# Seven products of half-size blocks instead of eight, in the projections of three images of a four-layer network

## The chip, the core and the metric

The kernel runs on one core of one Trainium2 chip. The core has an engine for matrix products (TensorE, called PE in the profile, with a separate path PEld that loads weights), three engines for elementwise work (VectorE or DVE, ScalarE or ACT, GpSimd or POOL), and a queue engine (SyncE or SP) that here only starts transfers. All engines run at the same time, each through its own list of instructions, in the order of that list, and wait for one another by semaphores. TensorE writes its results to PSUM, a small memory of eight banks per partition; one bank holds 512 numbers in fp32 per partition. GpSimd doesn't read PSUM in this kernel.

The metric is the device time of one execution in microseconds. Before the change it was 2751.64 us, the median of three runs (2740.83, 2752.58 and 2751.64).

## What is computed

The input is four images of 512 channels and 32 x 32 = 1024 positions (tokens), in fp32. Four layers follow one another, each `x = x + layer(group_norm(x))`: a self-attention with mixed heads, a gate per channel, a second self-attention (the one that is changed here), and a lookup of the eight best of 2048 stored items. Cut to the second self-attention, the reference says:

```python
def _conv1x1(x, w, b):
    return jnp.einsum('bchw,oc->bohw', x, w) + b[None, :, None, None]
# x: 4 images, 512 channels, 32 x 32; NUM_HEADS = 8, D_K = 64
q = _conv1x1(x, Wq, bq)
k, v = jnp.split(_conv1x1(x, Wkv, bkv), 2, axis=1)
q, k, v = (t.reshape(b, NUM_HEADS, D_K, l) for t in (q, k, v))
attn = jax.nn.softmax(jnp.einsum('bhct,bhcs->bhts', q, k) * SCALE, axis=-1)
out = jnp.einsum('bhts,bhcs->bhct', attn, v).reshape(b, c, h, w)
out = _conv1x1(out, Wp, bp)
```

So each image needs four products of a 512 x 512 weight with a 512 x 1024 image: the projections Q, K, V before the attention and P after it.

## The kernel before

Layer 2 (the second self-attention, counted from zero) takes the images one after another. Image 0 gets its Q, K and V at the end of layer 0; for the other three they are made between two attentions. One product of a projection is 128 output rows by 512 columns, summed over four blocks of 128 channels in PSUM:

```python
def project(w, rhs, m, at, evacuate, name="proj"):
    ps = place(at, f"{name}_{m}")              # two banks of PSUM
    for n in range(T // NB):                   # T = 1024, NB = 512
        for k in range(KC):                    # KC = 4
            pin(nc.tensor.matmul(
                ps[:, n, :], w[:, k, m * P:(m + 1) * P], rhs(k, n),
                start=(k == 0), stop=(k == KC - 1)))
    evacuate(flat2(ps))
# Q: q = (ps + bq) * SCALE on VectorE     K: k = ps + bk on ScalarE
# V: v = ps + bv on VectorE, with bv2 = bv copied to all partitions
```

That is 4 x 2 x 4 = 32 matmuls for each projection. `pin` keeps an instruction in its place in the program; instructions without it may be moved by the scheduler of the kernel language.

The attention of an image goes in 16 units of four key blocks:

```python
def scores2(b, u, before=None):
    # four times: two matmuls -> sc (two banks), then exp2():
    #   e = places2[:, count[0] % 6]; nc.scalar.activation(e, sc, AF.Exp)
    # the third and fourth exp come within apply2 of the unit before
    # sums of the e tiles for the softmax denominators:
    #   nc.gpsimd.tensor_add(two, es[i], es[i + 1])
    #   nc.vector.tensor_add(I["es", m, n], I["es", m, n], two)
def apply2(b, u, exp2=None):   # eight matmuls v x e -> pv
def finish2(b):                # after two units: rs matmuls, copy, reciprocal, o = pv * ri
```

The way out of the layer, P, adds the residual, which has to come from DRAM in pieces of 128 x 512:

```python
def put_out2(b):
    def add_out(m, ps):
        st = small.tile([P, 2, 6], F32, tag="bnst", ...)
        for n in range(T // NB):
            xr = apool.tile([P, NB], F32, tag="xr", bufs=2, ...)
            nc.sync.dma_start(out=xr, in_=x1[b][:, m, n * NB:(n + 1) * NB])
            nc.scalar.activation(xr, xr, AF.Identity, bias=I["tb"]..., scale=s1...)
            nc.vector.tensor_add(xr, ps[:, n * NB:(n + 1) * NB], xr)
            nc.sync.dma_start(out=x2[b][:, m, n * NB:(n + 1) * NB], in_=xr)
            nc.vector.bn_stats(st[:, n, :], xr)
        nc.vector.bn_aggr(mv[:, m, :], ...)
    for m in range(KC):
        project(I["Wp"], tokens(I["o"]), m, None, lambda ps: add_out(m, ps), ...)
```

Only two pieces `xr` exist, so a third is loaded when the first has been stored. The order of the whole layer, with its buffers:

```python
ps_s = tc.tile_pool(name="ps_s2", bufs=3, space=PSUM)   # three tiles of two banks
ps_m = tc.tile_pool(name="ps_m2", bufs=2, space=PSUM)   # two tiles of one bank, for pv
# ... memT (the items of layer 3, 4 MB) is loaded here, before layer 2 begins
for b in range(B):
    for s, u in enumerate(UNITS2):                 # 16 units
        if s == 5 and not last: load2(b + 1)       # Wq, Wk, Wv of the next image
        if s >= 1: scores2(b, u, UNITS2[s - 1])
        # steps of the normalization of the next image (from s == 8) ...
    if not last:
        for m in range(KC): take_q2(b + 1, m)      # Q
        img[b]["Wp"] = load_w("Wp", ...)
    apply2(b, UNITS2[-1])
    if not last:
        for m in range(KC): take_k2(b + 1, m)      # K
    finish2(b)
    if not last:
        for i in range(TC // 2): take_v2(b + 1, i) # V
        scores2(b + 1, UNITS2[0])                  # first unit of the next image
    put_out2(b)                                    # P
```

The weights Wq, Wk, Wv and Wp share three places of 1 MB, taken in turn.

Of the kernel before, what the change touches and what calls it, by code (L numbers as in the profile page):

```python
# [16 lines left out]
P = 128  # L17
# [24 lines left out]
def fast_net(ctx: ExitStack, tc: tile.TileContext, a: dict, out: bass.AP, flag: bass.AP):  # L42
# [17 lines left out]
    def small_ps(name):  # L60
        return pt_bank
# [12 lines left out]
    bq2 = chan(a["bq"], "bq2")  # L74
    bk2 = chan(a["bk"], "bk2")
    bp2 = chan(a["bp"], "bp2")
    fcb = chan(a["fc_b"], "fcb")

    both = const.tile([P, C], F32, tag="fcw", name="fcw")
# [814 lines left out]

    count = [0]

    def prepare2(b, in_steps=False):
# [31 lines left out]
    def take_q2(b, m, at=None):  # L931
        I = img[b]
        if m == 0:
            I["q"] = big("q", f"q2_{b}")
        project(I["Wq"], tokens(I["xn"]), m, at, lambda ps: pin(nc.vector.tensor_scalar(
            I["q"][:, m, :], ps, bq2[:, m:m + 1], SCALE, ALU.add, ALU.mult)), f"q2_{b}")

    def take_k2(b, m, at=None):
        I = img[b]
# [5 lines left out]
    def take_v2(b, i, at=None):  # L945
        I = img[b]
        if i == 0:
            I["v"] = big("v", f"v2_{b}").rearrange("p k (i c) -> p (k i) c", c=C)
        project_tokens(
            I["Wv"], lambda k, t: I["xn"][:, k, t * P:(t + 1) * P], i, at,  # L950
            lambda ps: pin(nc.vector.tensor_add(
                I["v"][:, 2 * i:2 * i + 2, :], ps,
                bv2.rearrange("p c -> p () c").to_broadcast([P, 2, C]))), f"v2_{b}")

    def scores2(b, u, before=None):

# [7 lines left out]
        def exp2():  # L964
            e = places2[:, count[0] % 6]
            count[0] += 1
            nc.scalar.activation(e, scs[len(es)], AF.Exp)  # L967
            es.append(e)

        for i, t in enumerate(range(t0, t0 + 4)):  # L970
# [44 lines left out]
    def finish2(b):  # L1015
# [19 lines left out]
        for r in range(2):  # L1035
            i = 2 * ((b * KC + m) * (T // NB) + n) + r
            nc.gpsimd.dma_start(out=seen[i:i + 1, :], in_=ri[r * HD:r * HD + 1])

    def put_out2(b):
        I = img[b]  # L1040
        s1 = l2[b][1]
        mv = small.tile([P, KC, 2], F32, tag="mv", name=f"mv_d{b}")

        def add_out(m, ps):
            st = small.tile([P, 2, 6], F32, tag="bnst", name=f"st_d{b}_{m}")
            for n in range(T // NB):
                xr = apool.tile([P, NB], F32, tag="xr", bufs=2, name=f"xr_c{b}_{m}_{n}")
                nc.sync.dma_start(out=xr, in_=x1[b][:, m, n * NB:(n + 1) * NB])
                nc.scalar.activation(
                    xr, xr, AF.Identity, bias=I["tb"][:, m:m + 1], scale=s1[:, m:m + 1])  # L1050
                nc.vector.tensor_add(xr, ps[:, n * NB:(n + 1) * NB], xr)
                nc.sync.dma_start(out=x2[b][:, m, n * NB:(n + 1) * NB], in_=xr)
                nc.vector.bn_stats(st[:, n, :], xr)
            nc.vector.bn_aggr(mv[:, m, :], st.rearrange("p i s -> p (i s)"))

        for m in range(KC):
            project(I["Wp"], tokens(I["o"]), m, None, lambda ps: add_out(m, ps), f"p2_{b}")
        gc3 = const.tile([P, 2, KC], F32, tag=f"gc3_{b}", name=f"gc3_{b}")
        l3[b] = (mv, gc3)

# [189 lines left out]
    for b in range(B):  # L1250
# [22 lines left out]
            ks[m](at)  # L1273
        if last:
            run_out(instance_norm(b))
            bv2 = apool.tile([P, C], F32, tag="o2", name="bv2")
            nc.sync.dma_start(out=bv2, in_=a["bv"].partition_broadcast(P))
            for i, at in enumerate(("mx0", "mx1", "sc", "mx0")):
                take_v2(0, i, at)
            for m, at in enumerate(("mx1", "sc", "mx0", "mx1")):  # L1280
                put_out(b, m, at)
# [11 lines left out]
    places2 = eT_flat[:, 0:6 * 2 * NB].rearrange("p (i r q) -> p i r q", i=6, r=2)  # L1293
    sums2 = eT_flat[:, 6 * 2 * NB:8 * 2 * NB].rearrange("p (i r q) -> p i r q", i=2, r=2)
    pair_sum = e.rearrange("p i r qq k -> p i r (qq k)")
    memT = []
    for k in range(KC):
        if k < 2:
            m_ = apool.tile([P, NI], F32, tag="s2", bufs=2, name=f"memT{k}")
        else:  # L1300
            m_ = eT_flat[:, (4 + k) * NI:(5 + k) * NI]
        nc.sync.dma_start(out=m_, in_=a["memT"][k * P:(k + 1) * P, :])
        memT.append(m_)
    tiles = [(b, tt) for b in range(B) for tt in range(TC)]
    atts, picks, sums = {}, {}, {}
    scores2(0, UNITS2[0])
    for b in range(B):
# [4 lines left out]
        for s, u in enumerate(UNITS2):  # L1312
            if s == 5 and not last:
                load2(b + 1)
            if s == 5 and last:
                img[b]["Wp"] = load_w("Wp", f"Wp2_{b}")
            if s >= 1:
                scores2(b, u, UNITS2[s - 1])
            for _ in range(2):
                if s >= 3:  # L1320
                    next(behind, None)
                if s >= 8:
                    next(ahead, None)
        run_out(ahead)
        if not last:
            for m in range(KC):
                take_q2(b + 1, m)
            img[b]["Wp"] = load_w("Wp", f"Wp2_{b}")
        apply2(b, UNITS2[-1])
        if not last:  # L1330
            for m in range(KC):
                take_k2(b + 1, m)
        finish2(b)
        if last:
            atts[0] = attention(*tiles[0])
        else:
            for i in range(TC // 2):
                take_v2(b + 1, i)
            scores2(b + 1, UNITS2[0])
        put_out2(b)  # L1340

# [739 lines left out]
```

## Time and profile before

The profile is of one execution with a span of 2741.6 us. Line numbers (L...) are those of the kernel before.

| what | where in the profile | number |
|---|---|---|
| TensorE busy | first part of the page | 2593.0 us, 95% of the span |
| GpSimd busy | first part of the page | 1266.2 us, 46% |
| VectorE busy | first part of the page | 1522.8 us, 56% |
| one projection of 32 matmuls | chain of work, PE q, k, v L197/L209 | 27.66 us |
| from the start of Q to the first product of the values in the next image | chain of work, 1508.68 to 1641.24 | 132.6 us |
| the 16 units of an attention | chain of work, 1641.24 to 1745.93 | 104.7 us |
| sum of two e tiles on GpSimd, 128 x 1024 | groups of instructions, POOL L991 | 2412 ns |
| the same on VectorE | groups of instructions, DVE L992 | 1384 ns |

How to read it: the trace holds two records of a weight load and two of a matmul for each fp32 matmul of the program, so that a projection appears as 64 records. The chain of work is followed backwards from the last instruction of the program: at each step it goes to what released that instruction, or, if it waited for nothing, to the one before it on its engine. Where the chain stays on PE, only a shorter list of PE work makes the program shorter; where it leaves PE for a DMA or another engine, PE stood still.

### The profile page before, as it was taken

To read this page: it belongs to the slowest core of one execution; us is meant where nothing else is said; L and a number is where in the kernel's file an instruction comes from. 1 tells how busy PE (TensorE), PEld (TensorE's weight loads), DVE (VectorE), ACT (ScalarE), POOL (GpSimd) and SP (SyncE) were. 2 spreads that over 40 slices of the span, in tenths; PEclk is the share of its full clock that TensorE was granted. 3 is DMA by queue.
4 is the path that set the end of the run, shared out by engine and by line. 5 is a ranking of instruction groups with operands and counts; after the bars stand their busy time and mean duration, and the time that the engine had idled before them with its cause. 6 is when DMAs were issued, how large, how long until landed. Compare 5 with 4: busy or idle time off the path is not lost.

```text
span 2741.6 us, 46996 instructions
## 1 busy us (share of the span) xinstructions
PE 2593.0 (95%) x18286; PEld 1180.3 (43%) x18286; DVE 1522.8 (56%) x2386; ACT 1007.6 (37%) x1149; POOL 1266.2 (46%) x1955
## 2 busy tenths in 40 slices
PE   8988999989989898989999999999999999999995
PEld 3443544545445444545433433343343334444442
DVE  5487337871588526873235224513623537788886
ACT  0565336551565426552154025214502622121210
POOL 2266325552455514653067017305702735666664
PEclk9999999999999999999999999999999999999997
DMA  2577438880687627785310030021002016767665
GB/s 78 128 206 204 128 93 219 218 216 28 172 216 202 164 69 193 205 207 199 116 32 1 31 123 1 16 77 62 1 31 92 1 48 189 220 186 216 185 183 148
DMA packets 159321, 349.82 MB, mean 128 GB/s; under 512 B 32361, under 2 KB 65129, under 8 KB 155378
## 3 DMA queue, kind: packets, MB, share of 16 engines
q1 hardware_dynamic: 86304, 167.04, 21.2%
q0 software_dynamic: 51200, 142.93, 19.3%
q10 hardware_dynamic: 21586, 36.76, 4.6%
q8 instruction: 147, 2.41, 0.4%
q14 instruction: 84, 0.69, 0.1%
HBM read 178.57 MB, written 33.69 MB: 77 GB/s over the span
## 4 chain that ended last, share of the span: by engine, by line
PE 82%; DMA 7%; ACT 4%; DVE 2%; issue 1%; POOL 1%; SPq 1%; ACTq 0%; POOLq 0%; DVEq 0%
PE at L1094 16%; PE sc_c L973 7%; PE pv_c L1006 7%; PE sc L451 7%; PE mx L197 7%; PE pv L511 6%; PE pt L410 4%; DMA s<-ss 4%; PE p L197 4%; PE sc L197 4%; PE v L209 3%; PE k L197 3%; PE q L197 3%; PE pt L684 3%; ACT ss L457 2%; PE mx L471 2%
## 5 line engine op out<-in xcount | busy, mean ns | idle before, releaser
L484 DVE STREAM_TRANSPOSE eT<-e 128x1024 f32<-128x1024 f32 x256 | 317.6, 1242 | 273.9 <-ACT e L478 272.0
L464 POOL DMA_DIRECT2D s<-ss x512 | 259.8, 515 | 384.4 <-ACT ss L457 299.6
L1111 POOL DMA_INDIRECT got<-in_mem,ix x256 | 280.2, 1095 | 208.3 <-DVE tmx L1117 92.3
L457 ACT COPY ss<-sc 128x1024 f32<-128x1024 f32 x256 | 258.9, 1011 | 264.4 <-PE sc L451 212.7
L967 ACT ACTIVATE eT<-sc_c 128x1024 f32<-128x1024 f32 x256 | 247.9, 1021 | 275.3 <-PE sc_c L973 213.3
L500 DVE BATCH_NORM_STATS2 st<-e 128x6 f32<-128x256 f32 x1024 | 341.6, 406 | 0.0
L451 PE MATMUL sc<-k,q 64*32 64x512 f32 x4096 | 287.1, 617 | 22.5 <-ACT ss L457 17.6
L991 POOL TENSOR_TENSOR e<-eT 128x1024 f32<-128x1024 f32 x96 | 231.3, 2412 | 164.7 <-ACT eT L967 133.2
L478 ACT ACTIVATE e<-mx 128x1024 f32<-128x1024 f32 x256 | 262.5, 1029 | 65.5 <-PE mx L471 28.0
L992 DVE TENSOR_TENSOR eT<-eT,e 128x1024 f32<-128x1024 f32 x96 | 132.8, 1384 | 274.0 <-POOL e L991 274.0
L511 PE MATMUL pv<-eT,v 128*64 128x128 f32 x4096 | 256.5, 279 | 0.0
L973 PE MATMUL sc_c<-q,k 64*128 64x512 f32 x1024 | 243.2, 614 | 11.3 <-ACT eT L967 9.0
L511 PEld LDWEIGHTS pv<-eT,v 128*64 128x64 f32 x4096 | 226.1, 139 | 63.9 <-issue 62.3
L1006 PE MATMUL pv_c<-eT,v 128*64 128x512 f32 x1024 | 234.4, 600 | 0.0
L471 PE MATMUL mx<-s,wmix 32*32 32x512 f32 x4096 | 159.6, 625 | 45.0 <-DMA s<-ss 44.9
L1135 DVE SCALAR_TENSOR_TENSOR acc<-got,et,acc 128x512 f32<-128x512 f32 x224 | 168.4, 752 | 8.0
L1033 DVE RECIPROCAL ri_c<-ri_c 128x512 f32<-128x512 f32 x32 | 107.0, 3345 | 96.1 <-ACT ri_c L1032 96.1
L973 PEld LDWEIGHTS sc_c<-q,k 64*128 64x128 f32 x1024 | 94.9, 189 | 144.0 <-issue 74.7
L1099 ACT COPY att<-at 128x1024 f32<-128x1024 f32 x64 | 64.8, 1012 | 217.8 <-PE at L1094 217.6
L987 POOL TENSOR_TENSOR eT<-eT 128x1024 f32<-128x1024 f32 x32 | 76.0, 2374 | 147.0 <-ACT eT L967 146.8
L587 POOL TENSOR_TENSOR o<-pv,rb 64x256 f32<-64x256 f32 x128 | 111.1, 868 | 67.1 <-ACT pv L574 60.2
L1006 PEld LDWEIGHTS pv_c<-eT,v 128*64 128x64 f32 x1024 | 70.9, 138 | 155.2 <-issue 154.6
(317 smaller groups left out, 3325.5 us busy)
## 6 DMA issues: line engine op xcount, KB each, us to landing
s<-ss SPq DMA_DIRECT2D x512, 128.0 KB
s<-ss POOLq DMA_DIRECT2D x512, 128.0 KB, 4.4
rb<-r POOLq DMA_DIRECT2D x64, 128.0 KB, 5.9
o<-o SPq DMA_DIRECT2D x32, 256.0 KB
xr<-in_x ACTq DMA_DIRECT2D x32, 256.0 KB
x<-xr SPq DMA_DIRECT2D x32, 256.0 KB
xr_c<-x SPq DMA_DIRECT2D x32, 256.0 KB
x<-xr_c SPq DMA_DIRECT2D x32, 256.0 KB
```

The source lines that it names most:

```text
L197: pin(nc.tensor.matmul(ps[:, n, :], w[:, k, m * P:(m + 1) * P], rhs(k, n), start=(k == 0), stop=(k == KC - 1),))
L451: pin(nc.tensor.matmul(sc[m * NS:(m + 1) * NS, r, :], q[r * HD:(r + 1) * HD, m, s * NS:(s + 1) * NS], k_[r * HD:(r + 1) * HD, m, n * NB:(n ...
L457: pin(nc.scalar.copy(ss[:, :, n * NB:(n + 1) * NB], sc))
L464: pin(relays[r].dma_start(out=s2[r * KC + m::NH], in_=ss[m * NS:(m + 1) * NS, r, :]))
L478: pin(nc.scalar.activation(e[:, half].rearrange("p r qq k -> p (r qq k)"), flat2(pairs[f"mx{half}"]), AF.Exp))
L484: pin(nc.vector.transpose(eT[:, j % 2].rearrange("p b (qq i r) x -> p i r qq b x", qq=2, i=4)[:, i, 2 * half:2 * half + 2], e[:, half].rea ...
L500: pin(nc.vector.bn_stats(st[:, i, 2 * half + r, qq, :], e[:, half, r, qq, :]))
L511: pin(nc.tensor.matmul(pv[r * HD:(r + 1) * HD, gp, :], I["v"][:, t, g * HD:(g + 1) * HD], eT[:, j % 2, t, :, 4 * g:4 * g + 4], start=(t == ...
L973: pin(nc.tensor.matmul(sc[:, r, :], I["k"][r * HD:(r + 1) * HD, m, t * P:(t + 1) * P], I["q"][r * HD:(r + 1) * HD, m, n * NB:(n + 1) * NB] ...
L1006: pin(nc.tensor.matmul(pv[r * HD:(r + 1) * HD, :], I["v"][:, t, h * HD:(h + 1) * HD], e[:, r, :], start=(t == 0), stop=(t == TC - 1),))
L1094: pin(nc.tensor.matmul(sc[:, n * NB:(n + 1) * NB], xn3[b][:, k, tt * P:(tt + 1) * P], memT[k][:, i0:i0 + NB], start=(k == 0), stop=(k == K ...
L1111: pin(nc.gpsimd.indirect_dma_start(out=got[:, i, :], out_offset=None, in_=a["mem"], in_offset=bass.IndirectOffsetOnAxis(ap=ix[:, i:i + 1], ...
```

## The change

A product of 2 x 2 blocks can be had from seven products of blocks instead of eight, if sums of blocks are formed before and after (Strassen's form, here with the fifteen sums of Winograd's variant). The change uses this for the projections Q, K and V of the images 1 to 3 and P of the images 0 to 2. The weight is cut into four blocks of 256 x 256, the image into four of 256 x 512. The aim is fewer matmuls on TensorE: 28 instead of 32 for each projection. The sums of weight blocks go to GpSimd, those of image blocks and of results to VectorE.

Around it: SCALE moves from the evacuation of Q into the exp; the bias of V no longer is added to V but carried through Wp once (`carry_bias`, 16 small matmuls) into the bias of P; and the items of layer 3 are loaded late, since their place now holds sums of blocks. The core of the diff, cut where `...` stands:

```diff
+    def seven_w(w, nm):                     # blocks of 128 x (2 x 256) on GpSimd
+        s = apool.tile([P, NI], F32, tag="s2", bufs=2, name=f"s_{nm}")
+        s1, s2_, s4 = ( ... )
+        nc.gpsimd.tensor_add(s1, block(1, 0), block(1, 1))
+        nc.gpsimd.tensor_sub(s2_, s1, block(0, 0))
+        nc.gpsimd.tensor_sub(s4, block(0, 1), s2_)
+        nc.gpsimd.tensor_sub(block(1, 0), block(0, 0), block(1, 0))
+        return None, block(0, 0), block(0, 1), s4, block(1, 1), s1, s2_, block(1, 0)
+
+    def seven_x(x, places):                 # blocks of 128 x (2 x 512) on VectorE
+        t1, t2, t4 = places
+        nc.vector.tensor_sub(t1, block(0, 1), block(0, 0))
+        nc.vector.tensor_sub(block(0, 1), block(1, 1), block(0, 1))
+        nc.vector.tensor_sub(t2, block(1, 1), t1)
+        nc.vector.tensor_sub(t4, block(1, 0), t2)
+        return None, block(0, 0), block(1, 0), block(1, 1), t4, t1, t2, block(0, 1)
+
+    def seven(product, put, nm):
+        ag = ps_s.tile([P, 2, NB], F32, tag="sc", name=f"ag_{nm}")
+        de = ps_s.tile([P, 2, NB], F32, tag="sc", name=f"de_{nm}")
+        product(1, ag[:, 0], True)
+        u2 = apool.tile([P, NB], F32, tag="o1", name=f"u2_{nm}")   # one buffer
+        nc.scalar.copy(u2, ag[:, 0])
+        product(6, ag[:, 1], True)
+        nc.vector.tensor_add(u2, u2, ag[:, 1])
+        product(5, de[:, 0], True)
+        product(7, de[:, 1], True)
+        u3 = apool.tile([P, NB], F32, tag="o2", name=f"u3_{nm}")
+        nc.vector.tensor_add(u3, u2, de[:, 1])
+        put(1, 1, u3, de[:, 0])
+        product(2, ag[:, 0], False)
+        put(0, 0, None, ag[:, 0])
+        product(4, de[:, 1], False)
+        put(1, 0, u2, de[:, 1])
+        product(3, de[:, 0], False)
+        put(0, 1, u2, de[:, 0])
+
+    # seven_by_channels (Q, K, P): a product is two matmuls of 512 columns
+    # project7_tokens (V): a product is four matmuls of 256 columns
 ...
-            nc.scalar.activation(e, scs[len(es)], AF.Exp)
+            nc.scalar.activation(e, scs[len(es)], AF.Exp, scale=SCALE)
 ...
+    def carry_bias(b):                      # once, for b == 0
+        for m in range(KC):
+            for k in range(KC):
+                pin(nc.tensor.matmul(
+                    ps[:, m:m + 1], img[b]["Wp"][:, k, m * P:(m + 1) * P], bv2[:, k:k + 1], ...
 ...
     def put_out2(b):
+        nc.gpsimd.tensor_add(I["tb"], I["tb"], cb)
+        def add_out(m, n, u, ps):
+            xr = apool.tile([P, NB], F32, tag="xr", bufs=2, ...)
+            nc.sync.dma_start(out=xr, in_=x1[b][:, m, n * NB:(n + 1) * NB])
+            nc.scalar.activation(xr, xr, AF.Identity, bias=I["tb"]..., scale=s1...)
+            if u is None:
+                nc.vector.tensor_add(xr, ps, xr)
+            else:
+                y = apool.tile([P, NB], F32, tag="xs", ...)   # one buffer
+                nc.vector.tensor_add(y, u, ps)
+                nc.gpsimd.tensor_add(xr, xr, y)
+            nc.sync.dma_start(out=x2[b][:, m, n * NB:(n + 1) * NB], in_=xr)
+            nc.vector.bn_stats(sts[m][:, n, :], xr)
+        if b + 1 < B:
+            for m in range(2):
+                seven(seven_by_channels(I["A", "Wp"], I["O"], m), ...)
 ...
+            if s == 2 and last:
+                load_items()                # memT, before: ahead of layer 2
+            if s in (8, 9) and not last:
+                key = ("Wq", "Wk")[s - 8]
+                img[b + 1]["A", key] = seven_w(img[b + 1][key], ...)
 ...
-            for m in range(KC):
-                take_q2(b + 1, m)
+            J["X"] = seven_x(J["xn"], thirds(halves2))
+            take7(b + 1, "Wq")
+            J["A", "Wv"] = seven_w(J["Wv"], ...)
+            I["Wp"] = load_w("Wp", f"Wp2_{b}")
         apply2(b, UNITS2[-1])
         if not last:
-            for m in range(KC):
-                take_k2(b + 1, m)
+            take7(b + 1, "Wk")
+            if b == 0:
+                carry_bias(b)
+            I["A", "Wp"] = seven_w(I["Wp"], ...)
         finish2(b)
 ...
-            for i in range(TC // 2):
-                take_v2(b + 1, i)
+            rest = eight_k([P, 2 * T], f"t_o{b}")   # one of the three 1 MB places
+            I["O"] = seven_x(I["o"], [rest[:, 0:T], rest[:, T:2 * T], halves2[:, 3 * T:4 * T]])
+            take7(b + 1, "Wv")
             scores2(b + 1, UNITS2[0])
         put_out2(b)
```

Only `product` carries `pin`. The sums, the copies and the transfers may be moved.

## The prediction

> **What bounds the kernel now.** I read the page's busy times first, then the chain of work through one passage between two attentions (images 0 and 1), then ScalarE's timeline where that chain leaves TensorE. From the page:
>
> ```profile
> PE 2593.0 (95%) x18286; PEld 1180.3 (43%) x18286; DVE 1522.8 (56%) x2386; ACT 1007.6 (37%) x1149; POOL 1266.2 (46%) x1955
> PE 82%; DMA 7%; ACT 4%; DVE 2%; issue 1%; POOL 1%; SPq 1%; ACTq 0%; POOLq 0%; DVEq 0%
> ```
>
> TensorE is the bound: 95% busy and 82% of the chain. The passage (start in us, length in us, what):
>
> ```profile
> 1508.68 27.66 PE q L197 x64
> 1536.34 3.58 PE pv_c L1006 x16
> 1539.93 27.66 PE k L197 x64
> 1567.59 1.01 PE rs_c L1027 x4
> 1568.60 27.66 PE v L209 x64
> 1596.27 3.63 PE sc_c L973 x16
> 1599.90 27.68 PE p L197 x64
> ...
> 1628.38 6.05 DMA x<-xr_c
> ...
> 1634.48 3.05 DMA xr_c<-x
> ...
> 1637.64 0.54 ACT xr_c L1049
> ```
>
> Q, K and V stand on PE without a gap: what they lose in matmuls is won in time. P is different. Behind it the chain is a store, the load into the freed piece, and ScalarE. In ScalarE's timeline:
>
> ```profile
> 1632.31 1.94 ACT L967 ACTIVATE eT<-sc_c 128x1024 f32<-128x1024 f32 x2 [1.65 <-PE pv_c L1006]
> 1637.64 1.52 ACT L1049 ACTIVATE xr_c<-xr_c,tb,s 128x512 f32<-128x512 f32 x2 [3.38 <-DMA xr_c<-x]
> 1639.06 1.91 ACT L967 ACTIVATE eT<-sc_c 128x1024 f32<-128x1024 f32 x2
> ```
>
> ScalarE scales the first two pieces of the next image's P here, ahead of exps that PE needs. The exps go on at 1639.1, which is 42.8 us after V's end at 1596.27. So P is a chain of pieces, hardly shorter than its matmuls: inside P, ScalarE took a pair at 1613.0, 1619.9 and 1626.6, 6.8 us apart, while PE made a pair in 6.9 us.
>
> **What the Trainium skill says.** "PSUM — Partial Sum Buffer", section "Engine vs sequencer instructions": the queues of ScalarE, VectorE and GpSimd are strictly first in, first out. The trace agrees: the exp at 1639.06 had its scores ready and stood behind a wait for a DMA. All below rests on this. "SBUF — State Buffer", section "SBUF: two separate sides": a VectorE operation with two inputs in SBUF and a GpSimd operation that reads SBUF exclude each other. The trace fits without proving it: L992 on VectorE takes 1.23 us beside an idle GpSimd in the passage and 1384 ns in the mean. So I expect sums a little dearer than the shortest record. "DMA: Bandwidth & Descriptors", section "Queues, rings and completion order": on each DMA engine descriptors are consumed in ring order. Here the store issued at 1628.38, behind a 1 MB weight load issued at 1627.60, took 6.05 us; the same stores without one in front were followed by the next load 2.1 us after their issue (1607.72 to 1609.85).
>
> **The change, part by part.**
>
> *Q and K, all three images.* 28 of 32 matmuls remain: 27.66 x 28/32 = 24.20 us, so 3.46 us less each. The built kernel's order has the four VectorE sums of the image (128x1024, about 1.3 us each) inside the units before, GpSimd's sums of Wq and Wk well ahead of Q. Nothing else is on the path; each of VectorE's five operations per half (0.7 us, from L1051's 687 ns) fits in the half's 12.1 us. Six projections: -20.7 us.
>
> *V, three images.* Its matmuls have 256 columns, 56 of them, 112 records. In the trace eight such records (L684) last 2.00 us together and the last of them 0.379, so they start 1.62/7 = 0.231 us apart (against 0.432 for 512 columns), so V takes 112 x 0.231 = 25.9 us instead of 27.66. VectorE's list holds, ahead of V's third sum, a reciprocal (3345 ns), a product (0.68) and two or three of the sums of O (1.3 each): u3 comes at about 10 to 11 us after V's start, while PE asks for it at 8.9. I take 1.5 us for that wait: V wins 0.3 us, three times, -1 us.
>
> *carry_bias, once.* 16 matmuls of one column; the gate's (L863) took 1.05 us for four, the group norm's with 128 rows and four columns (L150) 0.32 from start to the next start. 16 x 0.28 = +4.5 us, all on the path.
>
> *P, three images: the disputed part.* I walked the built order of each engine from V's end as zero, with the durations of the trace. GpSimd first stands before the sums of the next image's Wq, though the source has them in unit 8: its load can begin only at V's end (it takes V's place) and needs about 4.5 us; four sums of 128x512, half of 2.4 us each, end at 9; two e sums end at 14. PE begins P at 3.6, its first result is on VectorE at 12.0, so piece one is added on GpSimd at 14 to 15. From there a pair of pieces needs store 2.1, load 3, ScalarE 0.8, GpSimd 1.2, then the second y (which has one buffer, so it waits for that sum) 1.4, GpSimd 1.2: some 10 us instead of 6.8. The second half's copy of u2 waits for the last y of the first half (24 us), so PE ends P at 30.7, where it was 31.3 before: of 3.46 us only 0.6 are left. Then GpSimd's list has the sums of the next Wk, ahead of the adds of the last pair. That load takes Wp's place, so it begins after P's last use of Wp, about 32, behind the 1 MB of Wv; it lands at 36.5, the sums end at 41.3, and only then come the last two adds (with e sums between, 46), their stores (48), the loads of the next image's first pair (51) and ScalarE's scaling (52). The exps go on at 52 instead of 42.8: +9 us. For image 2 there are no such weight sums, but the items' 4 MB stand in the same queue between stores and loads; I get about the same. Three passages: +27 us.
>
> *Start of layer 2.* Before, ScalarE waited for the first pair at 1380 and PE for the exps 2.77 us. Now the first pair waits for carry_bias, far later, and the items aren't loaded there: -3 us.
>
> *Units.* VectorE gets 4 x 1.3 us per attention beside 57 us in 105: some waits, +1 us each, +3.
>
> Sum: -20.7 - 1 + 4.5 + 27 - 3 + 3 = +10 us.
>
> **The rivals.** *A, only PE counts:* the waits I found don't add up as walked, since DMAs or sums come earlier; P wins its 3.46 too. Twelve projections of 3.46 would be -41.5; with carry_bias, the V term, and the start it is about -31 (-41.5 + 4.5 + 9.5 - 3), 2721 us. For it: PE is 95% busy and the passages lose only about 3 us each to waits now. Against it: the list of GpSimd, which is fixed. *B, GpSimd becomes the bound also inside the units:* it's busy 79.5 of 105 us there, and if weight sums or late e sums held back the six e places, each attention could lose 5 to 10 us more: 2780 us. Against it: the order shows that all sums of weights have moved out of the units. *C, the walked chain:* 2762 us.
>
> **Range and chances.** I give C about 0.65, A 0.25, B 0.1: 0.65 x 2762 + 0.25 x 2721 + 0.1 x 2780 = 2754; since A in full is the end of its side, I lean to C and say 2757 us. The three runs before differ by 12 us, each of three passages may be off by 6. The range is 2728 to 2785. Faster by 2% means 55 us, more than all the removed matmuls are worth (41.5): 0.03. Slower by 2% needs C and B together: 0.05. Within 2%: 0.92.
>
> **What would show each step right or wrong.** Right: Q and K each last 24.2 us on PE (56 records); V 26 to 28 with a short wait for VectorE in its first half; P has waits for ScalarE and VectorE in its second half and lasts about 27; after it PE waits some ten us for exps, and back through ScalarE, a load, a store and a GpSimd add the chain comes to the sums of Wk and to its load. From V's end to the first exps of the second unit after P it is 52 us, not 43. Wrong: if this stretch is 40 us or less, A holds. If waits of exps for GpSimd's e sums show within units 3 to 15, B does. If Q or K takes more than 25 us, evacuation through one u2 and one u3 is too slow, which I don't expect.

## The result, and the profile after

The changed kernel takes 2837.3 us (median of 4 runs, 2836.5 to 2844.6) against 2746.2 us of the kernel before (4 runs, 2737.1 to 2752.6): 1.034 times the time, 95% interval 1.030 to 1.038. It is slower by 91 us, and the prediction of 2757 us (2728 to 2785) was wrong.

The profile after is of an execution with a span of 2835.9 us, 94.3 us more than the one before. Line numbers are now those of the changed kernel. The first part of its page:

```profile
PE 2593.1 (91%) x18390; PEld 1199.3 (42%) x18390; DVE 1606.7 (57%) x2488; ACT 1022.2 (36%) x1180; POOL 1354.4 (48%) x2025
...
PE 27%; DVE 2%; POOL 1%; issue 1%; DMA 1%; ACT 0%; ACTq 0%; POOLq 0%; SPq 0%; DVEq 0%
```

TensorE's busy time is what it was (2593.0), though 48 matmuls' worth of 512 columns are gone: either they were not saved, or the rest became slower. The share fell from 95% to 91%, so idle time grew. The second line, the chain, is of little use this time: its shares add up to 32%, so it was followed back through the last third of the program only. The next place to look is what PE waits for, here in layer 2 alone (1370 to 2330 us); the columns are the sum of the waits in us, how many, and the longest:

```profile
PE sc_c L1091 <- ACT eT L1085: 23.3, 9, 6.5
PE ag_q L959 <- DVE u_q L942: 14.9, 3, 5.0
PE ag_p L959 <- ACT u_p L940: 11.7, 6, 3.8
...
PE de_k L959 <- DVE k L973: 5.0, 6, 0.8
...
PE ag_k L959 <- ACT u_k L940: 4.1, 6, 0.7
```

Before, layer 2 had no waits inside a projection. The last two rows are the surprise: K waits twelve times, twice in each half of each K, always for about 0.7 or 0.8 us. PE's timeline shows where; here the beginning of the first Q and the first half of the first K (start, length, operation, how many records, and in brackets the idle time in front and who ended it):

```profile
1513.81 1.98 PE L959 MATMUL ag_q<-xn_c,Wq 128*128 128x512 f32 x4
...
1526.92 3.78 PE L959 MATMUL ag_q<-xn_c,Wq 128*128 128x512 f32 x4 [5.04 <-DVE u_q L942]
1530.50 2.61 PE L959 MATMUL de_q<-eT,Wq 128*128 128x512 f32 x4
...
1553.63 1.98 PE L959 MATMUL ag_k<-xn_c,Wk 128*128 128x512 f32 x4
1556.29 1.98 PE L959 MATMUL ag_k<-eT,s_Wk 128*128 128x512 f32 x4 [0.68 <-ACT u_k L940]
1558.11 1.88 PE L959 MATMUL de_k<-eT,s_Wk 128*128 128x512 f32 x4
...
1566.10 1.98 PE L959 MATMUL de_k<-xn_c,s_Wk 128*128 128x512 f32 x4 [0.84 <-DVE k L973]
```

A product is four records and 1.72 us (1558.11 to 1559.83, the next start). The second product of K, number 6, waits for ScalarE's copy of product 1; but it writes bank `ag[:, 1]`, and the copy reads `ag[:, 0]`. The last, number 3, writes `de[:, 0]` and waits for VectorE's `put(1, 0)`, which reads `de[:, 1]`. No value and no place is shared: only the tile. The same two waits stand in every seven. Q has a third, of 5 us: product 2 writes `ag[:, 0]` and waits for VectorE's first add, which has not come yet. That add reads `ag[:, 1]`, so the tile is at work here too; but product 4, right behind, writes `de[:, 1]`, which VectorE's second add has to read first, and that came at 1526.97 only. So PE would have had to wait for VectorE one product later. Behind that wait the first eight records take 3.78 and 2.61 us instead of 1.98 and 1.88.

The passage's end, which the prediction followed on ScalarE, in the same view of ScalarE:

```profile
1669.26 1.02 ACT L1085 ACTIVATE eT<-sc_c 128x1024 f32<-128x1024 f32 x1 [0.17 <-PE pv_c L1124]
1675.24 0.81 ACT L1182 ACTIVATE xr_c<-xr_c,tb,s 128x512 f32<-128x512 f32 x1 [4.96 <-DMA xr_c<-x]
1676.76 0.81 ACT L1182 ACTIVATE xr_c<-xr_c,tb,s 128x512 f32<-128x512 f32 x1 [0.70 <-DMA xr_c<-x]
1677.48 1.92 ACT L1085 ACTIVATE eT<-sc_c 128x1024 f32<-128x1024 f32 x2
```

The exps go on at 1677.5, 59.6 us after V's end (1617.9): predicted were 52, before it was 42.8. And GpSimd's list in the same stretch:

```profile
1620.28 1.26 POOL L914 TENSOR_TENSOR s_Wq<-Wq 128x512 f32<-128x512 f32 x1 [28.07 <-DMA Wq<-in_Wq]
...
1627.59 2.36 POOL L1109 TENSOR_TENSOR e<-eT 128x1024 f32<-128x1024 f32 x1
1633.39 1.26 POOL L1189 TENSOR_TENSOR xr_c<-xr_c,y_c 128x512 f32<-128x512 f32 x1 [3.45 <-DVE y_c L1188]
...
1662.10 1.26 POOL L914 TENSOR_TENSOR s_Wk<-Wk 128x512 f32<-128x512 f32 x1 [8.14 <-DMA Wk<-in_Wk]
...
1667.11 1.27 POOL L1189 TENSOR_TENSOR xr_c<-xr_c,y_c 128x512 f32<-128x512 f32 x1
```

The sums of the next Wq and Wk stand where the prediction had read them from the built order, waiting for their loads, the second in front of P's last adds.

The whole difference by stages, each the sum over the three passages, from PE's timelines (us; "behind P" is from P's end to the second group of pv products of the next image, where the passage in the table of before ends; "units" are the attentions outside the passages, the last one up to its P):

| | Q | K | V | P | behind P | units | carry_bias and start |
|---|---|---|---|---|---|---|---|
| before | 83.0 | 83.0 | 83.0 | 83.0 | 39.8 | 456.5 | |
| after | 107.5 | 85.7 | 89.8 | 105.2 | 62.9 | 467.7 | 3.6 |
| difference | +24.5 | +2.7 | +6.8 | +22.2 | +23.1 | +11.2 | +3.6 |

The sum is 94.1 of the 94.3 us.

### The profile page after: what moved, and what is told of

The parts are those of the page before. It is cut to its first block, busy times and chain, and to the rows that moved or that the text cites. A ratio compares the mean times of both kernels' runs of the same rounds, so it can differ in the third digit from the quotient of the medians.

```text
span 2835.9 us, 47536 instructions
## 1 busy us (share of the span) xinstructions
PE 2593.1 (91%) x18390; PEld 1199.3 (42%) x18390; DVE 1606.7 (57%) x2488; ACT 1022.2 (36%) x1180; POOL 1354.4 (48%) x2025
## 5 line engine op out<-in xcount | busy, mean ns | idle before, releaser
L1110 DVE TENSOR_TENSOR eT<-eT,e 128x1024 f32<-128x1024 f32 x96 | 140.1, 1459 | 267.0 <-POOL e L1109 266.9
L452 PEld LDWEIGHTS sc<-k,q 64*32 64x32 f32 x4096 | 47.8, 106 | 188.1 <-ACT ss L458 145.3
L1105 POOL TENSOR_TENSOR eT<-eT 128x1024 f32<-128x1024 f32 x32 | 76.6, 2395 | 94.1 <-ACT eT L1085 93.8
## 6 DMA issues: line engine op xcount, KB each, us to landing
s<-ss SPq DMA_DIRECT2D x512, 128.0 KB
s<-ss POOLq DMA_DIRECT2D x512, 128.0 KB
rb<-r POOLq DMA_DIRECT2D x64, 128.0 KB
```

Of the source, the lines that this page charges most:

```text
L452: pin(nc.tensor.matmul(sc[m * NS:(m + 1) * NS, r, :], q[r * HD:(r + 1) * HD, m, s * NS:(s + 1) * NS], k_[r * HD:(r + 1) * HD, m, n * NB:(n ...
```

## The experiments

Theory 1: waits are kept for a PSUM tile as a whole, so that products wait for readers of the tile's other bank; VectorE late at Q adds to it. Theory 2, the prediction's: GpSimd's list with the sums of the weights of the next image is the loss. Theory 3: VectorE can't do five operations per half in time. Sums over the three passages as above; "ratio" is against the kernel before, with its interval:

| run | Q | K | V | P | behind P | units | time, us | ratio |
|---|---|---|---|---|---|---|---|---|
| before | 83.0 | 83.0 | 83.0 | 83.0 | 39.8 | 456.5 | 2746 | 1 |
| after | 107.5 | 85.7 | 89.8 | 105.2 | 62.9 | 467.7 | 2837.3 | 1.034 (1.030-1.038) |
| e1_emit | 97.4 | 73.4 | 77.7 | 89.7 | 61.2 | 465.7 | 2787.3 | 1.017 (1.015-1.018) |
| e2_tiles | 98.6 | 72.7 | 74.9 | 92.4 | 64.5 | 468.2 | 2793.1 | 1.017 (1.014-1.020) |
| e3_p_plain | 107.9 | 85.7 | 87.2 | 83.0 | 42.6 | 465.8 | 2787.2 | 1.017 (1.014-1.019) |
| e4_pin | 92.1 | 85.8 | 89.1 | 105.0 | 50.5 | 562.5 | 2905.5 | 1.059 (1.057-1.061) |
| e7_emit_pin | 82.1 | 73.4 | 77.7 | 85.6 | 51.9 | 562.0 | 2853.4 | 1.040 (1.037-1.042) |
| e7b_emit_pin | 95.7 | 73.4 | 78.4 | 83.6 | 55.3 | 513.8 | 2817.8 | 1.025 (1.021-1.029) |
| e12_pieces | 97.5 | 73.4 | 78.9 | 87.2 | 43.6 | 474.2 | 2776.4 | 1.010 (1.006-1.013) |
| e5_rest | 83.0 | 83.0 | 84.7 | 83.0 | 40.3 | 455.7 | 2751.2 | 1.001 (0.999-1.003) |
| e13_kv_pieces | 83.0 | 73.4 | 74.1 | 83.0 | 39.8 | 467.7 | 2746.6 | 1.000 (0.998-1.002) |
| e16_kept | 97.6 | 73.4 | 78.9 | 73.0 | 48.6 | 466.9 | 2758.5 | 1.005 (1.003-1.007) |
| e17_kv_kept | 83.0 | 73.4 | 74.0 | 83.0 | 39.6 | 465.6 | 2746.6 | 1.001 (0.999-1.002) |
| e18_k_kept | 83.0 | 73.4 | 83.0 | 83.0 | 38.5 | 465.4 | 2736.5 | 0.997 (0.996-0.998) |
| e19_pv_first | 82.9 | 73.1 | 78.5 | 73.0 | 48.6 | 477.1 | 2748.0 | 0.999 (0.998-1.000) |
| e20_kp_kept | 83.0 | 73.4 | 83.0 | 73.0 | 48.1 | 466.2 | 2743.4 | 0.998 (0.997-0.999) |

The scores between V and P (3.6 us in a passage before) are in no column: in e12, e13, e16, e17 and e19 they take 3.5 to 5.0 us more over the three passages. Layer 2's first product of values starts between 1379.8 and 1391.6 us in the profiles. No edit is meant for what lies before it, but the scheduler puts the first image's sums of weights there (in the changed kernel those of Wq at 1296.8 and of Wk at 1325.1). So the stages are compared within layer 2, and small differences of the time by the ratios.

### The two banks of one tile

*e1_emit*: only the order in which `seven` is written.

```diff
         product(1, ag[:, 0], True)
+        product(6, ag[:, 1], True)
         u2 = apool.tile(...)
         nc.scalar.copy(u2, ag[:, 0])
-        product(6, ag[:, 1], True)
...
         product(4, de[:, 1], False)
-        put(1, 0, u2, de[:, 1])
         product(3, de[:, 0], False)
+        put(1, 0, u2, de[:, 1])
         put(0, 1, u2, de[:, 0])
```

> Inside each seven, only the order of emission is changed: products 1 and 6 are both written before ScalarE and VectorE read either, and products 4 and 3 both before VectorE reads either. Same instructions, same data, same PSUM tiles. Theory 1 (the two banks of one PSUM tile are waited for together, so that products 6 and 3 wait for readers of the other bank): K goes from 28.5 us to 24.2 to 24.8 in all three images, V from 29.3-31.2 to 26-27.5, Q from 35.4-36.2 to 29-31 (its wait for a late VectorE is real and stays), and the time to about 2800. Theory 2 (the loss is GpSimd's list with the hoisted weight sums): K stays at 28.5, time 2830-2840. Theory 3 (VectorE is too late with its five operations per half): K stays above 27, its waits move to products 4 and 3 of the new order.

Measured: K 24.45 us in all three images, V 25.8 to 26.0, the time 2787 us. In PE's timeline of this run the first half of K (the second column is the length, and the brackets are gone):

```profile
1545.31 1.98 PE L959 MATMUL ag_k<-xn_c,Wk 128*128 128x512 f32 x4
1547.13 1.88 PE L959 MATMUL ag_k<-eT,s_Wk 128*128 128x512 f32 x4
1548.84 1.88 PE L959 MATMUL de_k<-eT,s_Wk 128*128 128x512 f32 x4
```

*e2_tiles*: the order as changed, but a tile for each of the four sums.

```diff
-        ag = ps_s.tile([P, 2, NB], F32, tag="sc", ...)
-        de = ps_s.tile([P, 2, NB], F32, tag="sc", ...)
+        a_, g_, d_ = (ps_s.tile([P, 2, NB], F32, tag="sc", ...)[:, 0] for c in ("ag", "gg", "de"))
+        # the fourth: a tile of the pool of pv, passed in as bank
```

> The changed kernel in its own order of emission, but each of a seven's four sums in a PSUM tile of its own (three tiles of the scores, of which one bank each is used, and one of the tiles of pv), so that no wait can be shared between two banks of a tile. Same instructions. If the loss inside the seven comes from waits kept for whole tiles, K goes from 28.5 to 24.2-24.8 us here too and the time to 2785-2800, as with the changed order of emission. If it was the order by itself (for example when ScalarE and VectorE get to the two banks), K stays at 27 us or more.

Measured: K 24.23 us, 2793 us. The order is as it was, only the tiles are apart, and K's waits are gone; the first three products again:

```profile
1550.86 1.98 PE L959 MATMUL ag_k<-xn_c,Wk 128*128 128x512 f32 x4
1552.68 1.88 PE L959 MATMUL gg_k<-eT,s_Wk 128*128 128x512 f32 x4
1554.40 1.88 PE L959 MATMUL de_k<-eT,s_Wk 128*128 128x512 f32 x4
```

Together the two runs show theory 1: in the built program these products waited for the readers of their tile, whichever bank those read. Q stays at 98.6 us in the sum, since its fourth tile is one of pv's: product 7 waits 5.4 to 7.0 us until VectorE has taken the last pv product out of that place. The Trainium skill ("PSUM — Partial Sum Buffer", section "PSUM bank collisions raise a hardware error") has the chip's own rule per bank: each bank of a partition is a memory of its own, and accesses of two engines must be kept apart within a bank. The runs agree: different banks needed no wait. Theory 3 falls for K: the same five VectorE operations per half are all in time.

### P, and GpSimd's list

*e3_p_plain*: P in eight products again, without the sums of O and Wp.

```diff
-        if b + 1 < B:
+        if False:                    # in put_out2: the plain project for all images
...
-            I["A", "Wp"] = seven_w(I["Wp"], ...)
...
-            rest = eight_k([P, 2 * T], ...)
-            I["O"] = seven_x(I["o"], [...])
```

> Q, K and V in seven products as changed; P again as eight products in the plain form, the sums of O and of Wp are left out. P's part: P lasted 34.3 to 36.3 us and PE waited 18.7 to 22.6 us behind it, before the change 27.7 and 12.3 to 13.8. If P in this form is the cause of both (theory 2 in the form in which it needs GpSimd's adds), P is 27.7 again and the wait behind it about 13: 45 us less in three images, time about 2792. If the wait behind P comes from the weight sums alone, which delay the e sums whatever P needs, only P's own 22 us come back: about 2815. Theory 1 says nothing of P's tail: K stays 28.5.

Measured: P 27.66 us, behind it 42.6 in the sum instead of 62.9, 2787 us. P in seven products cost 42 of the 94 us (22.2 + 20.3). The sums of the next Wk still stand in GpSimd's list at P's beginning here (1613.6), but delay P no more, since it no longer needs GpSimd.

*e4_pin* and *e7_emit_pin*: GpSimd's order held to that of the source, the second with the order of e1_emit.

```diff
-        nc.gpsimd.tensor_add(s1, block(1, 0), block(1, 1))
+        pin(nc.gpsimd.tensor_add(s1, block(1, 0), block(1, 1)))   # likewise all four sums,
+        # the adds to xr (L1189) and the sums of e (L1105, L1109)
```

> The sums of weights, the sums of e and the adds to P's pieces keep the order of the source on GpSimd, so that the sums of the next Wq and Wk no longer stand in front of P's adds. The number of instructions is the same. Theory 2 (those sums and their waits for loads are the loss): P shortens from 34-36 to about 28-30 and the wait of PE behind it from 19-23 to 13-16 us, time about 2800; K, Q, V unchanged. Theory 1: K 28.5, Q 35 and V 29-31 stay, and most of P's length too, since its products also wait for the other bank; then P is over 31 and the time 2815 to 2830.

> The order of emission of the first run and the pinned GpSimd order together. If the two causes are separate, their gains add: K 24.2-24.8, V 26-27.5, Q 29-31, P 26-29 with 13-16 us behind it; time about 2765 if each alone brings 37. If they are one and the same cause, the time is that of the better of the two alone.

Measured: 2905 and 2853 us, slower than the changed kernel. What was aimed at came about in part (behind P 62.9 to 50.5), but the units grew by 95 us, which no theory had. PE's waits for VectorE's adds of e (`rs_c <- DVE eT L1110`) grew from 7.1 us in layer 2 to 53.4, about half of it. Why VectorE is late shows in its groups of the second attention, here e4_pin and under it the changed kernel (busy time and mean ns of one, then the idle time in front):

```profile
L1110 DVE TENSOR_TENSOR eT<-eT,e 128x1024 f32<-128x1024 f32 x21 | 61.6, 2932 | 40.4 <-POOL e L1109 39.7
```

```profile
L1110 DVE TENSOR_TENSOR eT<-eT,e 128x1024 f32<-128x1024 f32 x20 | 27.3, 1363 | 47.3 <-POOL e L1109 47.3
```

The same add takes twice as long when GpSimd's sums of e come in pairs, so that each of VectorE's falls beside one; in the free order they mostly take turns. That fits the exclusion of which the prediction had seen 1.23 against 1384 ns. The runs were bad experiments for theory 2, since pinning the sums of e changed what they should have kept. Q became 15 us shorter in both (e7_emit_pin against e1_emit): in e4_pin VectorE came to Q's first add 9.1 us after Q's start, in the changed kernel 12.4.

*e7b_emit_pin*: e1_emit with only the sums of weights and the adds to xr pinned.

> The order of emission of the first run, and only the sums of weights and the adds to P's pieces in the order of the source on GpSimd (the e sums are free to move, as in the changed kernel), so the sums of the next Wq and Wk stand in the units and behind all adds of P. Theory 2 for what is left of P (30.5 us and 12 behind it in the first run): P 28 to 29 and 5 to 7 us behind it, 8 to 9 us less per passage, but the sums come back to the units; if these take them without waits, the time is about 2760, if each unit's attention grows by 5 us or more as when all sums were pinned, it is 2775 or more. Rival (store and load of the two xr pieces bound P): P stays at 30 and 10 to 12 behind it.

Measured: P 83.6 instead of 89.7, behind it 55.3 instead of 61.2, so 12 us won, and the units 48 us longer: 2818 us. That speaks for the sums of the weights as what delays P (the adds to xr are pinned too, so it isn't shown by this run alone), and their proper place in the units is no free place.

*e12_pieces*: e1_emit, and places for P's pieces.

```diff
-            xr = apool.tile([P, NB], F32, tag="xr", bufs=2, ...)
+            if i < 6 and b + 1 < B:          # i: number of the piece in this P
+                xr = halves2[:, i * NB:(i + 1) * NB]
+            else:
+                xr = apool.tile([P, NB], F32, tag="xr", bufs=2, ...)
```

> The order of emission of the first run, and six of P's eight pieces in places of their own (those of the image's sums, free once V has read them) instead of two places for all eight, so that a load no longer waits for the store of an earlier piece. GpSimd's list is as it was. If the walk through store and load in two places is what P and the exps behind it wait for: P 28 us or less and 4 to 7 us behind it, 8 us less per passage, about 2763. If GpSimd's hoisted sums are (theory 2): P stays at 30 and 10 to 12 us behind it, 2787.

Measured: behind P 43.6 instead of 61.2 us, but P itself 31.0 and 31.8 us in two passages (24.3 in the third, where no next image's sums stand in GpSimd's list), and the units 8 us longer: 2776 us. So each theory had one half: the wait behind P is the walk of two places through store and load, P's own length is not. That is GpSimd's list, by way of VectorE. In the changed kernel's timeline of VectorE:

```profile
1629.97 1.22 DVE L1110 TENSOR_TENSOR eT<-eT,e 128x1024 f32<-128x1024 f32 x1 [11.30 <-POOL e L1109]
1631.12 0.68 DVE L942 TENSOR_TENSOR u_p<-u_p,ag_p 128x512 f32<-128x512 f32 x1
```

VectorE stood 11.3 us before an add of e that waited for GpSimd's sum of e (1627.59), which stood behind the sums of Wq, which waited for their load. P's first add came only then, though its two products had been ready since 1626.

*e16_kept*: e12_pieces, and the sums of the four weights made once, in the first passage, and kept in DRAM.

```diff
+        if key in kept:
+            nc.sync.dma_start(out=s, in_=kept[key])
+        else:
             nc.gpsimd.tensor_add(s1, block(1, 0), block(1, 1))
 ...
-            nc.gpsimd.tensor_sub(block(1, 0), block(0, 0), block(1, 0))
+            nc.gpsimd.tensor_sub(s7, block(0, 0), block(1, 0))     # a fourth place in s
+            kept[key] = dram.tile([P, NI], F32, ...)
+            nc.sync.dma_start(out=kept[key], in_=s)
```

> All four projections in seven products, order of emission of the first run, six of P's pieces in places of their own, and the sums of the four weights made once, for the first passage, kept in DRAM and loaded in the two others, so that GpSimd has no sums of weights in passages 2 and 3 and none of the next image in front of P's adds. If these sums are what is left of P's loss and of the longer units: P 27 us with 4 to 6 us behind it, and the attentions of images 1 and 2 at 115 to 117 us instead of up to 123.6. Q keeps its wait for VectorE (31 to 33 us). Against before, per passage: Q +4.4, K -3.2, V -1.8, P -0.7, behind P +2; with carry_bias 4.5 and the units 2 each the time is about 2755. If the units stay as long as with the sums on GpSimd, 2770.

Measured: P 24.33 us in all three passages, 28/32 of 27.66 to 0.5%, and 2759 us; the attentions of images 1 and 2 lasted 119 and 118 us from the first pv on, where 115 to 117 were expected. In the second P products 5, 7 and 2 follow one another so, where in the changed kernel product 2 (the third line) waited 2.17 us for VectorE:

```profile
1852.89 1.88 PE L967 MATMUL de_p<-t_o,s_Wp 128*128 128x512 f32 x4
1854.61 1.88 PE L967 MATMUL de_p<-eT,s_Wp 128*128 128x512 f32 x4
1856.33 1.88 PE L967 MATMUL ag_p<-eT,Wp 128*128 128x512 f32 x4
```

With the hoisted sums gone nothing is left of the loss inside P. Behind P it is 48.6 us, 5.0 more than in e12_pieces and 8.8 more than before; what causes that stays open.

### Q

*e19_pv_first*: e16_kept, with the products of the last unit ahead of Q.

```diff
+            apply2(b, UNITS2[-1])
             take7(b + 1, "Wq")
 ...
-        apply2(b, UNITS2[-1])                # now only for the last image
```

> The kernel with all four projections in seven products and the kept sums of weights, with one edit more: the pv products of the attention's last unit are emitted ahead of Q instead of behind it. If Q's first half waits because VectorE still has the last unit's reciprocal and e sums ahead of Q's first add, 3.6 us of pv in front of Q take that much of the wait: Q from 32.2-32.9 to 28-29.5 us, with a wait of up to 3 us of the pv products for their exps in front, so 0 to 4 us less per passage, 2747 to 2758. If Q's wait is made inside Q (its own two operations in a row, whatever lies before), Q stays at 32 and the time at 2759.

Measured: Q 25.4, 28.8 and 28.8 us instead of 32.8, 32.6 and 32.1, and the time 2748 us, no longer to be told from before (0.9975 to 1.0003). The pv products, which the rows of units now hold (10.8 us in three passages), did not wait for their exps. The reason for Q's wait, in VectorE's timeline of the changed kernel at the first Q:

```profile
1517.99 3.35 DVE L1110 TENSOR_TENSOR eT<-eT,e 128x1024 f32<-128x1024 f32 x1 [2.53 <-POOL e L1109]
1521.26 3.34 DVE L1151 RECIPROCAL ri_c<-ri_c 128x512 f32<-128x512 f32 x1
1524.53 1.16 DVE L1110 TENSOR_TENSOR eT<-eT,e 128x1024 f32<-128x1024 f32 x1
1525.60 0.67 DVE L1152 TENSOR_TENSOR eT<-pv_c,ri_c 128x512 f32<-128x512 f32 x1
1526.20 0.67 DVE L942 TENSOR_TENSOR u_q<-u_q,ag_q 128x512 f32<-128x512 f32 x1
```

Q starts at 1513.8; its first add comes at 1526.2, behind 12 us of the attention's leftovers, among them a wait of 2.53 us for GpSimd. So for Q theory 3 holds in another form: not the length of VectorE's five operations makes PE wait, but what stands in front of them.

### What pays

*e5_rest*: no sums, no sevens, the rest of the change.

```diff
-            take7(b + 1, "Wq")
+            for m in range(KC):
+                take_q2(b + 1, m)           # likewise K, V and P; no seven_w, no seven_x
```

> Control: all four projections as eight products again and no sums of weights or images; what is left of the change is V's bias carried into the last one (carry_bias), the scale in the exp, the late load of the items and the earlier start of the preparation. Prediction's terms: carry_bias +4.5 us, the start of layer 2 -3 us, so 2745 against 2744 before. If these side changes carry a part of the loss (VectorE or ScalarE late in the units), the time is above 2755 and the first attention stays near 128 us instead of 123.

Measured: 2751 us, 1.001 of before; the side changes are no part of the loss, and the first attention lasts 122.5 us again instead of 128.0.

*e13_kv_pieces*, *e17_kv_kept*: K and V in seven; the second keeps their sums as in e16_kept. *e18_k_kept*: K alone, without `carry_bias`. *e20_kp_kept*: K and P. All four keep the order of e1_emit and the places of e12_pieces; e20_kp_kept also gives y two places.

```diff
-            take7(b + 1, "Wq")
+            for m in range(KC):
+                take_q2(b + 1, m)           # e18, e20: V plain too; e13, e17, e18: P plain
+        t7 = ...                            # the image's seventh sum has a place of its own,
+        # so that Q reads the image as it is
-            if b == 0:
-                carry_bias(b)               # e18, e20: V's bias is added to V again
```

> Only K and V in seven products (the order of emission of the first run), Q and P plain, six of P's pieces in places of their own, the image's seventh sum in a place of its own too, so that Q can read the image unchanged. Sums that are left out: those of Wq, Wp and O. From the first run K 24.5 and V 25.9, against 27.7 each: -5 us per passage; Q 27.7 without waits for VectorE, P 27.7; carry_bias +4.5; P's wait behind it 3.6 as before or less. Time 2744 - 15 + 4.5 = 2734, less the relief of P's pieces if this was worth something before the change too (up to 9 us per passage). If the sums themselves cost the units 2 us each on GpSimd and VectorE, 2740.

> K and V in seven products as in the fourth run of the second set, Q and P plain, the sums of Wk and Wv made once and loaded afterwards. Passages stay at 118 us (4.7 less than before). If GpSimd's sums were what made the attentions 3 to 5 us longer, these are back at 115 to 117 us for images 1 and 2 and the time is 2733 to 2738 against 2745. If VectorE's sums of the image are, they stay at 119 and the time at 2745.

> Only K in seven products, its sums of Wk made once and loaded afterwards; V plain with its bias added as it is taken, so that carry_bias is left out. K 24.5 instead of 27.7: -3.2 us per passage, no 4.5 us for carry_bias. Image sums on VectorE stay in the units (1.4 us per attention by the run with K and V). Time 2745 - 9.6 + 4 = 2739; if VectorE's sums cost 3 us or more per attention, no gain.

> K and P in seven products, Q and V plain, V's bias added as it is taken (no carry_bias), six of P's pieces in places of their own, the sums of Wk and Wp made once and kept. From the two runs before: K 24.5 and P 24.4 us instead of 27.7, so -6.5 per passage; behind P 5.4 instead of 3.6; and the sums of O on VectorE in V, which may delay V's taking or P's start by 1 to 3 us; the units +2 to 5 as with K alone. K alone gave 0.9969 of the time before; with P another 0 to 4 us for each of three passages less: 2727 to 2738.

Measured: 2747, 2747, 2736 and 2743 us. K alone (0.9956 to 0.9981) and K with P (0.9969 to 0.9992) beat the kernel before, by 0.3% and 0.2%. In all of these the projections win 10 to 20 us together, but the units are 9 to 11 us longer than before, whether the weights' sums are made on GpSimd (467.7) or loaded (465.6); without the image's sums they aren't (455.7). In e17 and e18 PE waits five times in the units for VectorE's adds of e; here layer 2 of e17 (1385 to 2330 us, the columns as above):

```profile
PE rs_c L1153 <- DVE eT L1118: 7.0, 5, 2.8
PE gate L864 <- POOL zr L860: 2.4, 1, 2.4
```

Neither e5_rest nor the kernel before has a wait of either kind there. So VectorE's sums of the image are what is left to explain the longer units; no run has them alone. The rest of the gain goes to carry_bias and the scores between V and P (e13, e17), and in e20 to 8.3 us behind P. Of e18's 10 us the stages in layer 2 show 2 (passages -10.9, units +8.9), and the earlier start of layer 2, which e5_rest has too, (1379.8 and 1381.0 against 1385.7), is the rest of the profile's 7.9. Since that start differs among kernels that are alike up to there, it stays open how much of the 0.3% is K's. A version that beats both kernels is there; that K in seven products makes it so isn't shown: K's 9.6 us and the units' 8.9 nearly cancel, and the other 1.3 us lie behind P, where the pieces have other places.

## Why the prediction was wrong, point by point

*Q and K* were to win 20.7 us and lost 27.2 (+24.5 and +2.7): 48 of the 84 us by which the sum of the terms missed the profile. The step that failed: "Nothing else is on the path; each of VectorE's five operations per half (0.7 us, from L1051's 687 ns) fits in the half's 12.1 us." The sum of durations fits, as K shows in e1_emit. What failed is the step from durations to waits. Within each half, products were made to wait for readers of the tile's other bank: e1_emit took 12.3 us off K and 10.1 off Q, so 22 of the 48. The other 25 are Q's, 97.4 us in e1_emit where 72.6 were predicted: the prediction counted VectorE's operations in the half and not where VectorE is when Q begins. Of these e19_pv_first brought back 14.7 (97.6 to 82.9). The prediction named its own sign, "If Q or K takes more than 25 us, evacuation through one u2 and one u3 is too slow, which I don't expect": the sign came, with another cause. u2 and u3 still have one buffer each in e19_pv_first.

*V* was to win 1 and lost 6.8. The two-bank waits are the cause (12.1 us by e1_emit). The 1.5 us for VectorE were of about the right size by luck. In e1_emit one wait of 1.2 to 1.3 us is left in each passage, here in the second, and under it VectorE:

```profile
1834.48 1.99 PE L983 MATMUL de_v<-Wv,eT 128*128 128x256 f32 x8 [1.16 <-DVE v L996]
1832.01 0.68 DVE L946 TENSOR_TENSOR u_v<-u_v,de_v 128x512 f32<-128x512 f32 x1
1833.74 0.68 DVE L996 TENSOR_TENSOR v<-u_v,de_v 128x512 f32<-128x512 f32 x1
```

V started at 1824.4. u3 (L946) was there 8.3 us later, in time for product 4, which was due at 8.7; what product 4 waited for is `put(1, 1)` (L996), which reads the other bank of its tile. With the tiles apart (e2_tiles) V has no wait at all. The matmuls were taken too dear: 0.231 us a record gave 25.9, and without waits V takes 24.4 us (e2_tiles, the second and third image), 0.218 a record.

*carry_bias*: 4.5 predicted, 3.6 measured on PE.

*P*: the walk was right in its mechanism (hoisted sums, GpSimd's adds, store, load, ScalarE), and too short. Predicted +27, measured +45.3. The two ends it named came later: the exps 59.6 us after V's end, not 52. P, which was to end 0.6 us earlier, took 7.4 longer on average. The first piece was added on GpSimd 15.5 us after V's end (1633.4), where the walk had 14 to 15; what the walk left out is that PE's own products wait meanwhile, for the tile (the order of e1_emit took 15.5 us off the three) and for VectorE's first add behind the e sum (2.2 us in the first P, 4.8 in e12_pieces).

*Start of layer 2*: -3 predicted. The wait of 2.77 us is gone, but the stage before ended later by as much; nothing is to be concluded from one profile.

*Units*: +3 predicted, +11.2 measured; the mechanism, VectorE's sums of the image, is the one that the last runs show, and 5.1 of the 11.2 fall in the first attention.

*The rivals.* A gave 2721, B 2780, C 2762; the result lies above all three. Every one of them took 24.2 us for Q and K as given, so the range had no case in which the matmuls saved did not turn into time. The least probable branch was "Slower by 2% needs C and B together": it came by a fourth way.

## What to carry to other kernels

When results are taken out of PSUM in parts, give each part a tile of its own, or write all banks of a tile before the first is read: in these runs waits followed tiles, not banks. A stage's demands on another engine are to be laid on that engine's list at the time when the stage begins, not compared with the stage's length. And a cut in the bound engine's work needs a walk of the new order with every wait written down, before its full worth is put into a sum.

## What the runs showed of the hardware

After its longer waits PE was slower for some us. In e1_emit, around Q's wait, by stretches (columns: length; busy us and records of PE, PE's weight loads, VectorE, ScalarE, GpSimd; granted clock; DMA share; GB/s):

```profile
1509.70:1516.70 7.00, 7.00 (x18) 2.95 (x16) 4.48 (x3) 0.59 (x1) 4.65 (x2) 1.00 0.00 0
1521.30:1527.70 6.40, 6.38 (x8) 2.71 (x9) 1.44 (x2) 0.69 (x1) 0.00 (x0) 0.54 0.01 3
1527.80:1541.00 13.20, 13.20 (x32) 5.79 (x31) 3.53 (x5) 1.27 (x2) 0.00 (x0) 1.00 0.00 0
```

The eight records after the wait of 4.50 us ran at a granted clock of 0.54 and took 3 us more than such records do; so a wait of 4.5 us cost 7.5. The Trainium skill ("TensorE: Matmul & The Clock Gate", section "HAM oscillation — how this bites in real kernels") warns of idle gaps above about 3.4 us, after which the clock is cut. This trace agrees for 4.5 us, but as a threshold the runs don't show the figure. A wait of 2.12 us was followed by the lower clock (0.61 from 2127.1 to 2131.5 in e1_emit), one of 2.21 us was not (1.00 from 1631.8 to 1637.3 in the changed kernel). First e1_emit, then the changed kernel:

```profile
2127.16 3.01 PE L959 MATMUL ag_p<-eT,Wp 128*128 128x512 f32 x4 [2.12 <-DVE u_p L942]
1631.85 1.98 PE L959 MATMUL ag_p<-eT,Wp 128*128 128x512 f32 x4 [2.21 <-DVE u_p L942]
```

The slower clock is one reason why PE's busy time did not fall with the matmuls; how much of it was not measured. Shorter waits, of 0.68 to 0.84 us, were followed by records of nearly the usual length (1.98 for 1.88).
